# Decoder on one core: the MLP's second products by seven block products, four of them moved into the next slot

## The chip, the cores and the metric

The kernel runs on one core of a Trainium2 chip. The metric is the device time of one execution in microseconds (us). Of the kernel before there are three runs, and one more execution that was taken by the hardware profiler. The engines are called as the profile calls them: PE (TensorE, matrix products and transposes), PEld (its weight loads), DVE (VectorE), ACT (ScalarE), POOL (GpSimd) and SP (SyncE, which only issues DMAs here).

## The reference

`x` has the shape (8, 256, 256): 8 batches of 256 tokens with 256 features, all in float32. Cut to what matters:

```python
x0 = x
for i in range(4):
    x = x + self_attention(layer_norm(x, g1[i], b1[i]), Wq[i], Wk[i], Wv[i], Wo[i], bo[i])
    h = layer_norm(x, g2[i], b2[i])
    x = x + (gelu(h @ W1[i] + bias1[i]) @ W2[i] + b2_[i])     # 256 -> 1024 -> 256
x = layernorm(x0 + x)
x = layernorm(x + cross_attention(x, context, xWq, xWkv, xWout, xbout))
C1 = compose(fc1_logits, fc1_A, fc1_B)    # weighted sum of 32 low-rank products, 256 x 1024
C2 = compose(fc2_logits, fc2_A, fc2_B)    # the same, 1024 x 256
x = layernorm(x + gelu(x @ C1) @ C2)
```

Four of the eight heads of the self-attention are local (a causal softmax over a window of 128), and four are linear (softmax of q, elu + 1 of k, sums over buckets of 64). Cross-attention has 16 heads of 64 and 120 context tokens for each batch.

The part that the change touches is the product of `gelu(...)`, 256 x 1024, with `W2`, 1024 x 256, for each batch and layer. It is called the second product below, and the one with `W1` is the first product.

## The kernel before, in words

**Units and slots.** The work is cut into units of one batch and one layer: attention units 0 to 31 and MLP units 0 to 31, then 8 units of cross-attention and 8 units `Composed` of the last MLP. A unit keeps its batch's `x` (two tiles of 128 tokens by 256 features) in SBUF. The main loop (L1365 to L1496) has slots s = 1 to 32. A slot interleaves the second half of attention unit s-1 (`old`), the first half of attention unit s (`new`), MLP unit s-4 (`ff`), and the normalisation and transposition for attention unit s+1 (`after`). In slots 1 to 12 the composed weights are made as well. When they are done, in slot 13, the pools of that work are closed and a pool `cross` is opened; `filled` is true up to there. A second loop (L1506 on) runs cross-attention unit s beside an MLP unit or a `Composed` unit, up to s = 10: MLP units 29 to 31 for s = 0 to 2, `Composed` units 0 to 7 for s = 3 to 10.

**What sets the order.** Each engine runs its own queue in the order in which the program issues instructions; nothing reorders them. So the order of the calls in the loop is the order on each engine, and it is written out by hand. Waits between engines are put in by the framework from the tiles that are read and written. A tile is taken from a pool with a fixed number of buffers, and taking one waits until the buffer's last readers are done. PSUM has eight banks, four in `ps_s` (`bank_s`, L168) and four in `ps_g` (`bank_g`, L171).

**A slot's steps, by line.**
- `qkv` of `new` (L687): q and k transposed (L693, copies on ACT at L701 and on DVE at L702); then, for each of the two tiles w, k, q and v (L713), the copy of v on ACT (L720), the maximum of q and its subtraction on DVE (L725, L726), and the parts of elu + 1 of k on DVE (L732, L733). Between w = 0 and w = 1 it calls `between`; in before that is the normalisation of the next MLP unit (`centre`, L195).
- `linear_sums`, `divide_c`, `turn_p` and `values` of `old` (L809 to L893): the linear heads' sums, the transposes of the softmax weights `p` (L860) with their copies on ACT and, for the last head, DVE (L863, L865), and the products with v.
- `turn` and `turn_sums` of `ff`: transposes of the normalised x (L214), scale and shift on DVE (L223) and ACT (L224), and sums `tx` on POOL (L574 to L577).
- `scores` of `new` (L735): the products (L744), then on DVE for each head the causal mask (L753) and two row maxima (L757).
- The first product of `ff`. It already goes by seven block products in before: with 2 x 2 blocks for both factors, seven products of blocks and some sums of blocks give what eight products give. A block product is four matmuls 128x128 with 128 columns (`one`, L593). `p16`, `p5`, `p27`, `p34` (L608 to L636) are products 1 and 6, 5, 2 and 7, 3 and 4, with their copies (L612, L620, L622), the adds L614, L628 and L633 on DVE and the GELUs on ACT (L918), which end with four blocks `h[11]`, `h[12]`, `h[21]`, `h[22]` of 128 features x 4 x 128 tokens. `first_sums` forms the sums of the blocks of `W1` once for each layer on POOL (L560 to L563).
- `out` of `old` (L895): the projection (L239) and its addition to x (`add_to`, L231, L233).
- The exponentials of `new`: of `qs` and `ke` (L763, L764), then two for each head (`head_exps`, L769, L775). ACT loads a table when it changes from GELU to the exponential or back.
- The second product of `ff` (`second`, L638, L645): 8 matmuls 128x256 for one token tile (`second(1)`), the transposes for `after`, 8 matmuls for the other tile (`second(0)`), and then one addition to x on DVE (L233).
- `softmax_q`, `totals` and `divide` of `new` (L784 to L807), all on DVE: elu + 1 of k (L786), the softmax of q (L788 to L790), the reciprocals of the sums of `p` (L799, L800) and four divisions, one for each head (L805).

`add_bias` (L229) adds a bias to x on POOL. `moments` and `centre` are the two halves of a layer norm: mean and variance on DVE with the reciprocal root on POOL (L189), and the normalisation on DVE (L195). `load_attn` and `load_mlp` issue the weights' DMAs of the next layer on ACT's queue. In the second loop `Pair` makes keys and values of the context by seven products, `Cross` has the attention itself, and `Composed` is an MLP unit with composed weights, whose result is normalised one tile at a time and sent out on SP's queue (L973, L976).

In the names of tiles in the profile, `_a` is an attention unit, `_m` an MLP unit, `_f` a Composed unit; `x`, `h`, `p`, `qs`, `kf` are the tensors named above. A float32 matmul shows as two MATMUL records in the trace, a transpose as one.

## Time and profile before

| | us |
|---|---|
| runs of the kernel before | 1213.03, 1210.98, 1212.82 |
| median | 1212.82 |
| the profiled execution, by its own time | 1211.44 |
| its span in the profile | 1209.7 |
| first qk matmul of slot 13 / of slot 31 | 413.5 / 873.3 |
| length of a slot between these (18 slots) | 25.4 in most, 25.5 on average |
| first cross slot begins | 937.6 |
| length of a cross slot, s = 3 to 7 | 28.6 |

The rows of the profile read as follows. A line of a timeline has the start and the length in us of a run of neighbouring instructions, the engine, the line in the kernel, the operation, what it writes and reads, the shape and the number of instructions; in brackets stands the idle time before it and what ended that. A line of the table of windows has a stretch of the span, and then the busy time of each engine in it.

### The profile page before, as it was taken

How to read it: one execution, taken by the hardware profiler on the slowest of the kernel's cores; microseconds unless marked ns; L12 is line 12 of the kernel's file. 1: busy time of each engine (PE TensorE's matmuls, PEld its weight loads, DVE VectorE, ACT ScalarE, POOL GpSimd, SP SyncE). 2: the span in 40 equal slices, each digit the busy share in tenths (PEclk: the TensorE clock that was granted, in tenths of full speed). 3: DMA queues.
4: the chain of work that ended last, by engine and by line, in shares of the span. 5: the costliest groups of instructions: out<-in, count | busy, mean ns of one | idle time of the engine just before them, and what ended most of it. 6: DMA issues, size and time to landing. Idle time of an engine off the chain costs nothing. (4 is left out here: it accounts for less than half of the span.)

```text
span 1209.7 us, 24149 instructions
## 1 busy us (share of the span) xinstructions
PE 1193.1 (99%) x9117; PEld 956.4 (79%) x9117; DVE 867.1 (72%) x2446; ACT 645.9 (53%) x1794; POOL 457.7 (38%) x687
## 2 busy tenths in 40 slices
PE   8999999999999999999999999999999999999998
PEld 5556788888888888887888878888877777777797
DVE  6878788777878777777877777787774556666643
ACT  4444555554445567766667666677663343333323
POOL 6665455555564322222422222243234324232220
PEclk9999999999999999999999999999999999999999
DMA  5624131110310030010001002020000000000000
GB/s 160 209 85 120 45 92 46 32 31 27 119 45 1 16 111 2 1 47 29 2 1 40 1 2 75 2 70 27 10 10 1 10 9 16 21 9 9 9 15 23
DMA packets 29508, 47.83 MB, mean 40 GB/s; under 512 B 3151, under 2 KB 22735, under 8 KB 29135
## 3 DMA queue, kind: packets, MB, share of 16 engines
q0 software_dynamic: 6656, 20.98, 6.0%
q10 hardware_dynamic: 13024, 14.07, 3.5%
q1 hardware_dynamic: 9710, 11.23, 3.0%
q8 instruction: 72, 1.18, 0.4%
q14 instruction: 46, 0.37, 0.1%
HBM read 44.17 MB, written 2.10 MB: 38 GB/s over the span
## 5 line engine op out<-in xcount | busy, mean ns | idle before, releaser
L645 PE MATMUL ps_p_m<-w,h_m 128*128 128x256 f32 x1024 | 233.3, 380 | 0.0
L645 PEld LDWEIGHTS ps_p_m<-w,h_m 128*128 128x128 f32 x1024 | 189.2, 190 | 22.8
L229 POOL TENSOR_TENSOR x<-x,b 128x256 f32<-128x256 f32 x64 | 48.3, 775 | 221.0 <-DVE xn_m L195 221.0
L713 PE MATMUL qkv_a<-wa,xT_a 128*128 128x512 f32 x256 | 115.1, 592 | 0.0
L775 ACT ACTIVATE p_a<-sc_a,nm_a 128x128 f32<-128x128 f32 (+1 forms) x256 | 103.9, 431 | 2.2 <-DVE nm_a L757 2.0
L713 PEld LDWEIGHTS qkv_a<-wa,xT_a 128*128 128x128 f32 x256 | 48.6, 190 | 47.6 <-issue 45.9
L757 DVE TENSOR_REDUCE nm_a<-sc_a 128x1 f32<-128x128 f32 (+1 forms) x256 | 79.6, 352 | 4.4
L918 ACT ACTIVATE h_m<-h_m,cols 128x128 f32<-128x128 f32 x256 | 78.4, 406 | 0.0
L229 POOL TENSOR_TENSOR x<-x,bo 128x256 f32<-128x256 f32 x64 | 48.2, 774 | 73.3 <-DVE xn_a L195 73.3
L300 POOL DMA_INDIRECT ga<-in_L_ffn_fc_A_dram,idx_a x64 | 62.2, 973 | 24.0 <-issue 15.6
L596 PE MATMUL ps_h_m_a<-xT_m,w 128*128 128x128 f32 x512 | 70.6, 281 | 0.5 <-DVE xT_m L223 0.5
L720 ACT COPY v<-qkv_a 128x256 f32<-128x256 f32 x64 | 23.9, 373 | 84.4 <-PE qkv_a L713 84.4
L596 PE MATMUL ps_h_m_u<-tx_m,w 128*128 128x128 f32 x512 | 67.7, 275 | 0.0
L596 PEld LDWEIGHTS ps_h_m_a<-xT_m,w 128*128 128x128 f32 x512 | 62.4, 191 | 5.3 <-issue 1.9
L239 PE MATMUL ps_p_a<-wo,oT_a 128*128 128x256 f32 x256 | 65.6, 381 | 0.0
L805 DVE TENSOR_TENSOR p_a<-p_a,psum_a 128x384 f32<-128x384 f32 x128 | 63.8, 560 | 1.1
L596 PEld LDWEIGHTS ps_h_m_u<-tx_m,w 128*128 128x128 f32 x512 | 62.3, 192 | 0.0
L693 PE MATMUL ps_qk_a<-xT_a,wa 128*128 128x256 f32 x256 | 60.7, 380 | 0.9 <-ACT aw L354 0.9
L645 PE MATMUL ps_p_f<-w2c,h_f 128*128 128x256 f32 x256 | 57.8, 379 | 0.0
L753 DVE TENSOR_TENSOR sc_a<-sc_a,causal 128x256 f32<-128x256 f32 x128 | 54.3, 424 | 3.3 <-PE sc_a L744 2.1
L387 PE MATMUL ps_w<-gbt,at 128*128 128x512 f32 x128 | 56.7, 596 | 0.0
L775 ACT ACTIVATION_READ_ACCUMULATOR p_a<-sc_a,nm_a 128x1 f32 x256 | 55.9, 218 | 0.0
(312 smaller groups left out, 2742.1 us busy)
## 6 DMA issues: line engine op xcount, KB each, us to landing
w<-in_L_attn_W_dram ACTq DMA_DIRECT2D x8, 1024.0 KB, 6.3
xwkv<-in_L_xattn_Wkv_dram SPq DMA_DIRECT2D x1, 2048.0 KB, 10.2
x_c<-in_x_dram SPq DMA_DIRECT2D x8, 256.0 KB, 2.7
out_dram<-y_f SPq DMA_DIRECT2D x16, 128.0 KB, 1.7
x<-in_x_dram ACTq DMA_DIRECT2D x6, 256.0 KB, 3.5
ga<-in_L_ffn_fc_A_dram,idx_a POOLq DMA_INDIRECT x64, 3.4
xwq<-in_L_xattn_Wq_dram SPq DMA_DIRECT2D x1, 1024.0 KB, 4.8
xwo<-in_L_xattn_Wout_dram SPq DMA_DIRECT2D x1, 1024.0 KB
```

What stands on the lines that cost most here:

```text
L229: nc.gpsimd.tensor_add(xb[:, i, :], xb[:, i, :], bias)
L239: nc.tensor.matmul(ps[:, i * D : (i + 1) * D], lhs(c, i), w[:, c, :], start=c == 0, stop=c == n_in - 1,)
L300: nc.gpsimd.indirect_dma_start(out=dst, out_offset=None, in_=table, in_offset=bass.IndirectOffsetOnAxis(ap=idx, axis=0),)
L387: nc.tensor.matmul(ps, self.at[k][:, m * P : (m + 1) * P], self.b[k][:, n * 512 : (n + 1) * 512], start=k == 0, stop=k == PG - 1,)
L596: nc.tensor.matmul(ps[:, f * P : (f + 1) * P], self.ws[n][:, f * P : (f + 1) * P], self.rhs[n], start=start and f == 0, stop=stop and f == ...
L645: nc.tensor.matmul(self.ps[:, i * D : (i + 1) * D], self.h[k][:, f, :], self.w2[:, half * 4 + f, :], start=k in (11, 22) and f == 0, stop= ...
L693: nc.tensor.matmul(ps[s], wa[:, c, s * HW : (s + 1) * HW], xT[:, c, :], start=c == 0, stop=c == NC - 1,)
L713: nc.tensor.matmul(t, xT[:, c, w * P : (w + 1) * P], wa[:, c, 2 * HW :], start=c == 0, stop=c == NC - 1,)
L757: nc.vector.tensor_reduce(self.nmax[:, h, w : w + 1], sc[:, s], AX.X, ALU.max, negate=True)
L775: nc.scalar.activation(flat[:, s], sc[:, s], AF.Exp, bias=self.nmax[:, h, w : w + 1], accum_out=self.psum[:, h, w : w + 1],)
L805: nc.vector.tensor_tensor(p, p, self.psum[:, h, :, None].to_broadcast([P, 3, P]), ALU.mult)
L918: nc.scalar.activation(dst[:, f, :], src[:, f * P : (f + 1) * P], AF.Gelu, bias=col("ff", i))
```

## The change

The second product also goes by seven block products in slots 13 to 32, and beside cross-attention for s = 0 to 7: 28 units. The last three Composed units keep `second`, and so do the MLP units of slots 4 to 12. Besides that, the order of the calls is changed around it:

- `second_plain` makes products 1, 4 and 2 in one bank, from the GELU blocks as they are, with the transposes for `after` between 4 and 2. `h_sums` forms four sums of the blocks of h on POOL (128 x 512 each); `w2_sums` forms four sums of the blocks of `W2`, once for each layer, on POOL.
- `take` adds a finished block from PSUM to x on DVE, where before there was one addition for the unit. One block can go to two places of x.
- `second_56` and `second_73`, the products that need the sums, come in the next slot: 6 and 5 between the halves w = 0 and w = 1 of `qkv`, 7 and 3 after w = 1. In slot 32 and in the second loop they have other places, in a cross slot after `out`.
- `softmax_q`, `totals` and `divide` move from the end of the slot into the next slot's `qkv`, behind `second_56`.
- The exponentials of `qs` and `ke` come after those of the heads. The normalisation of the next MLP unit goes from `qkv` to the slot's end. The second half of `xT` for `after` is made on DVE and no longer on ACT. Products 5, 2, 7, 3, 4 of the first product are issued without `out` between them; `out(0)` and `out(1)` follow.
- The banks of `ps_s` are taken in a fixed turn; the bank for q and k comes from `ps_g`.
- In the second loop normalisation and transposes for the next unit come earlier, and Composed units 0 to 4 are sent out with one DMA for both tiles.

```diff
+        def two(self, n, ps, slot, a, start=False, between=None):
+            for f in range(4):
+                nc.tensor.matmul(
+                    ps[:, slot * P : (slot + 1) * P],
+                    a[:, f, :],
+                    self.w2s[n][:, f, :],
...
+        def take(self, blocks, src):
+            x = xs[self.b].rearrange("p i (n d) -> p (i n) d", n=2)[:, blocks, :]
+            nc.vector.tensor_add(x, x, src)
+        def second_plain(self, turn=None, between=None):
+            h = self.h
+            self.ps = bank_g(f"ps_p_{self.name}")
+            self.two(1, self.ps, 0, h[11], True, between)
+            self.two(4, self.ps, 2, h[22], False, between)
+            if turn:
+                turn()
+            self.two(2, self.ps, 1, h[12], False, between)
+        def h_sums(self):
...
+            nc.gpsimd.tensor_add(s1, h[21], h[22])
+            nc.gpsimd.tensor_sub(s2, s1, h[11])
+            nc.gpsimd.tensor_sub(h[21], h[11], h[21])
+            nc.gpsimd.tensor_sub(h[22], h[12], s2)
+            self.hs = {5: s1, 6: s2, 7: h[21], 3: h[22]}
+        def second_early(self):
+            ps = self.ps.rearrange("p (k d) -> p k d", k=4)
+            self.take(slice(0, 1), ps[:, 0:1, :])
+            self.take(slice(0, 3, 2), ps[:, 1:3, :])
+        def second_56(self):
...
+            self.two(6, ps, 0, hs[6])
+            self.take(slice(1, 2), ps[:, None, :P])
+            self.two(5, pd, 0, hs[5], start=True)
+            self.take(slice(3, 4), pd[:, None, :P])
+        def second_73(self):
...
+            self.two(7, ps, 0, hs[7])
+            self.take(slice(2, 4), ps[:, None, :P].to_broadcast([P, 2, P]))
+            self.two(3, pd, 0, hs[3])
+            self.take(slice(1, 2), pd[:, None, :P])
...
         if new and s > 1:
-            new.qkv(nxt_c)
+            def between():
+                late.second_56()
+                old.softmax_q()
+                old.totals()
+                old.divide(range(HL))
+            new.qkv(between if late else None, bank_g if late else bank_s)
+        if late and new:
+            late.second_73()
...
-        if ff:
-            ff.second(1, vsums and (lambda: next(vsums)))
...
+        if cross:
+            ff.w2s = w2s
+            ff.second_plain(after and (lambda: after.turn(alone=True)), vsums and (lambda: next(vsums, None)))
+            ff.h_sums()
+            if ff.b == B - 1:
+                mlp_sums[ff.l + 1] = first_sums(mlp_ws[ff.l + 1][0])
...
+        if new and cross:
+            new.begin_exps()
+            new.head_exps(range(HL))
+            new.exps()
...
-        if nxt_m and after and not filled:
-            nxt_c = nxt_m.centre
-        elif nxt_m:
+        if nxt_m:
             nxt_m.centre()
-        if ff:
+        if cross:
+            late = ff
+            ff.second_early()
+        elif ff:
             ff.second(0)
```

## The prediction

> **What bounds the kernel now.** I read the page first, for the span and the engines' shares; then the table of windows over a slot of self-attention, one of cross-attention, the passage between them and the tail; then the timelines of DVE, ACT and PE over the slot that begins at 642.8, because a share doesn't say who waits for whom.
>
> ```profile
> span 1209.7 us, 24149 instructions
> PE 1193.1 (99%) x9117; PEld 956.4 (79%) x9117; DVE 867.1 (72%) x2446; ACT 645.9 (53%) x1794; POOL 457.7 (38%) x687
> ```
>
> ```profile
> 642.80:668.20 25.40, 25.40 (x223) 21.05 (x223) 19.07 (x58) 17.09 (x52) 6.26 (x11) 1.00 0.14 44
> 1054.00:1082.60 28.60, 28.60 (x149) 21.72 (x148) 18.45 (x49) 9.65 (x16) 9.16 (x19) 1.00 0.06 19
> ```
>
> The second fence is the table of windows: after the window come its length and then PE, PE weight loads, DVE, ACT and POOL busy, and the granted clock. PE is without a gap in both kinds of slot, at a granted clock of 1.00. So PE seems to set the time, and an edit that takes work from PE to gain it, as long as nothing else closes in the same 25.4 us. DVE and ACT (19.07 and 17.09 us) look free; whether they are is seen only in order of time.
>
> ```profile
> 643.73 0.17 DVE L799 COPY psum_a<-psum_a 128x4 f32<-128x4 f32 x1 [2.23 <-ACT p_a L775]
> 644.19 1.96 DVE L805 TENSOR_TENSOR p_a<-p_a,psum_a 128x384 f32<-128x384 f32 x4
> 646.08 0.68 DVE L233 TENSOR_TENSOR x<-x,ps_p_m 128x512 f32<-128x512 f32 x1
> 646.67 0.41 DVE L702 COPY qk_a<-ps_qk_a 128x256 f32<-128x256 f32 x1
> ...
> 647.92 0.72 DVE L195 TENSOR_SCALAR xn_m<-x,mv_m,rs_m 128x256 f32<-128x256 f32 x2
> ...
> 655.70 0.69 DVE L614 TENSOR_TENSOR ps_h_m_u<-ps_h_m_u,h_m 128x512 f32<-128x512 f32 x1
> ...
> 665.44 0.42 DVE L786 TENSOR_TENSOR kf_a<-kf_a,ke_a 128x256 f32<-128x256 f32 x1
> ...
> 669.11 0.17 DVE L799 COPY psum_a<-psum_a 128x4 f32<-128x4 f32 x1 [2.22 <-ACT p_a L775]
> ```
>
> ```profile
> 656.42 0.59 ACT L620 COPY h_m<-ps_h_m_u 128x512 f32<-128x512 f32 x1 [1.83 <-DVE ps_h_m_u L614]
> ...
> 663.39 1.28 ACT L763 ACT_TABLE_LOAD   x1
> 664.68 0.42 ACT L763 ACTIVATE qs_a<-qs_a 128x256 f32<-128x256 f32 x1
> ...
> 666.90 0.57 ACT L224 ACTIVATE xT_a<-ps_t_a,cols 128x256 f32<-128x256 f32 x1
> ...
> 668.84 0.24 ACT L775 ACTIVATION_READ_ACCUMULATOR p_a<-sc_a,nm_a 128x1 f32 x1
> ```
>
> Here is a second closed ring. The last exponential of the heads (ACT, L775) releases the totals (DVE, L799) at 643.73. DVE has no gap over 0.2 us until the add L614 ends at 656.38: 12.65 us. That add releases the ACT copy L620 at 656.42, and from there ACT runs without a gap through the GELUs, the change of table and the exponentials to 669.08, and releases the next totals at 669.11: 12.69 us. 12.65 + 12.69 and the handover give 25.38, PE's own period. So two rings have the same length, and taking work from PE gains only if the other becomes shorter too.
>
> **What PE gains.** A unit's old second products are 16 matmuls 128x256 (each two records):
>
> ```profile
> 659.99 1.06 PE L596 MATMUL ps_h_m_u<-tx_m,w 128*128 128x128 f32 x8
> 660.88 3.62 PE L645 MATMUL ps_p_m<-w,h_m 128*128 128x256 f32 x16
> ```
>
> From start to start, 16 records of 256 columns take 3.46 us (660.88 to 664.34), so 16 matmuls take 6.92; 8 records of 128 columns take 0.89 (659.99 to 660.88), so the 28 matmuls 128x128 of seven products take 6.23. PE gains 0.69 us for a unit, and a slot of PE's alone would be 25.38 - 0.69 = 24.69. The 24 more weight loads of a unit cost nothing more, as the first products, all of the small kind, hold 0.89 with theirs.
>
> [...]
>
> **What the DVE part of the ring becomes.** In the changed order the ring is no longer closed by the totals. DVE's copy of qk (L702) waits for ACT's half of the same copy (L701), and ACT's order puts that behind the eight head exponentials and behind the exponentials of qs and ke, which were moved to the end. So DVE's part of the ring runs from the qk copy to the end of L614. Against the 12.65 us:
> - Out: the add L233 of the second products, 0.59 (646.08 to 646.67); the normalisation xn_m, 0.69 (647.92 to 648.61, now at the slot's end); the small wait before the masks, which is filled, 0.17.
> - In: the additions of products 6, 5, 7 and 3. Three are 128x128 from PSUM, 0.21 each by the spacing of L726, which has that size; one is 128x256, 0.34 by the spacing of L702: 0.97.
> - In: the four instructions of softmax_q (L786 to L790), now between the two halves of qkv. In before they lie beside ACT's exponentials, where DVE waits anyway (2.22 us in the last DVE row). Their spacing from 640.05 is 0.34 + 0.45 + 0.24 + 0.34 = 1.37.
>
> Sum: 12.65 - 1.45 + 0.97 + 1.37 = 13.54, so 0.89 more.
>
> **What the ACT part becomes.** Out: the second half of xT_a, 0.45 (666.90 to 667.35), now on DVE in a place where it waits for ACT anyway. The last exponential's accumulator read and its signal (668.84 to 669.11, 0.27) are no longer at the end; the qk copy is, 0.38 and 0.03 for the signal. Sum: -0.31. The qs and ke exponentials only change places.
>
> **The new period** is 25.38 + 0.89 - 0.31 = 25.96 us, against 24.69 for PE alone. PE then has 1.27 us of gaps in a slot; I expect them before product 7, which waits for DVE's addition of product 6 (same bank), and before ps_t_m, which waits for the addition of product 3.
>
> **The sum over slots 13 to 30** (first qk matmul from 413.5 to 873.3 us, 459.8 in all; mean 25.54, since slots 14, 18 and 26 wait 0.47 for a bank and 28 to 30 carry 1.6 of work on the context):
> - 18 x 25.96 = 467.3. I count the three bank waits as gone, since PE has gaps now.
> - Work on the context in slots 28 to 30: 0.6, as part of 1.6 now lies in PE's gaps.
> - POOL beside DVE. The sums of h (four POOL 128x512 a unit, 1.29 each by L433's mean in the page) and the bias addition behind them (1.51) end near softmax_q, whose first and last instructions read two operands in SBUF. Bounds for a slot: nothing, if they end before, and 0.4, if both instructions and one division lose what the rows below show. I take 0.1, as the overlap is short: 1.8 in all.
> - Slots 19 and 27: first_sums (4 POOL 128x512 at 1.27 to 1.36, 5.2 us) now stand behind the sums of h, and so beside the divisions and ahead of the bias addition. Bounds 0.9 (four divisions) and 2.5 (half of the 5.2 in PE's way): 1.5 each, 3.0.
> - Slots 13 and 21: the seven DMA issues of load_attn, on ACT's queue, took from 641.10 to 644.60. Nothing waited for them; now the qk copy stands behind them. They began 2.5 us before the last exponential ended, so about 1.0 is left over: 2.0. The three issues of load_mlp (some 1.5) fit into those 2.5.
> - Slot 13: w2_sums (four POOL 128x512, 5.2 us) start behind compose.final, which ends at 420.2; the sums tx of the MLP then come at about 425.5 to 426.6, and product 6 needed them at 424.4. Between 0.5 and 2.2: 1.4.
>
> 476.1 against 459.8: **16.3 us lost**.
>
> ```profile
> 900.95 2.83 DVE L805 TENSOR_TENSOR p_a<-p_a,psum_a 128x384 f32<-128x384 f32 x4
> ```
>
> This is the nearest row for POOL beside DVE: while POOL forms tx (L576 and L577, 0.77 us instead of 0.46), the four divisions take 2.83 us instead of 1.96, so 0.22 each.
>
> [...]
>
> **What is gained elsewhere.**
> - Cross slots: eight units at 0.69 = 5.5. PE is gapless there (28.60 of 28.60), and DVE and ACT (18.45 and 9.65) have room: the additions add 0.4, the sums 5.2 us to POOL's 9.16 of 28.60.
> - From slot 31 to the first cross slot (873.3 to 937.6), PE is busy for 61.73 of 64.3. Two units save 1.4 there, but slot 31 still has the long ring; some of the gaps are filled by the matmuls moved there. Net 0 to 2.5: 1.2.
> - The tail from 1168.4: the last Composed units get their transposes and first products earlier; gaps of 0.42 and some of 0.2 before products 4 and 7 go: 1.2 of 41.3 (0 to 2).
>
> That is 7.9 us. **Sum:** 16.3 - 7.9 = 8.4 over the profiled execution, 1211.44 (span 1209.7, 1.7 around it): 1219.8, so 1220. The median of the runs shown is 1212.82, 1.4 higher; on that scale it would be 1221.
>
> **The rivals.**
> - *The ring is 25.96, but its company is hidden* (POOL's sums, the DMA issues, slot 13). Then 467.3 + 0.6 - 459.8 - 7.9 = +0.2: 1211.6, no change. For it: most of these terms have nothing as a lower bound. Against it: the DMA issues stand on ACT, through which the ring runs.
> - *PE stays the bound, and the kernel is faster.* The place is the qk copy of DVE. If it isn't held by ACT's copy, because ACT gets there early or the wait is void, then the copy, the first half's four instructions and the first two additions (0.34 + 0.91 + 0.42) lie beside the exponentials; DVE's part is 11.87 and the ring about 24.3, below 24.69. It decides from there: as soon as the ring is under 24.69, each period is PE's. 18 x 0.69 = 12.4, less slot 13's 1.4, and with the 7.9: 18.9 less, 1192.5. Against it: ACT has no gap between L620 and the last exponential, and the copy is behind them all.
> - *The ring lies in between*, since starts of neighbouring instructions move closer in another order. At 25.4 to 25.6 it is 457 to 461, with 3 us of the extra terms: 1204 to 1208.
> - *More waits than I count*: product 6 waits for POOL's second sum, which I put at 1 us before it is needed, and each division loses time to POOL in every slot. At 0.6 us more a slot the time is 1220 + 11 = 1231.
>
> **Chances.** The forecast (1214 to 1226) 0.50; its company hidden 0.14; PE the bound 0.12; in between 0.12; more waits 0.12. Faster by over 0.2% (the 2.4 us that a measurement of this kernel can tell from no change) is 0.24, within it 0.14, slower 0.62. The range runs from 1201, which leaves out PE as the bound, to 1233, which takes in most of the last rival; the likeliest case's own range is 1214 to 1226.
>
> **What would show it.** Right: a period of 25.9 to 26.3 us between first qk matmuls of slots 14 to 30; PE gaps of about 1.3 us in a slot, before product 7 and ps_t_m; DVE's L702 waiting for ACT, then DVE without gaps to the add of p16; cross slots of 27.9. Wrong: PE gapless in slots 14 to 30 with a period near 24.7, or PE waiting for POOL before product 6. If the period is 25.96 and the total is not, the terms of single slots were mis-sized.

## The result

The changed kernel is **slower**: 1251.61 us (median of 1252.12, 1251.41, 1251.80 and 1248.09) against 1212.07 us for the kernel before on the same chip (four runs). The ratio is 1.0325, with a 95% interval of 1.0312 to 1.0337. The forecast was 1220, with a range from 1201 to 1233, so the sign was right and the size was a fifth of what came: +8.4 was worked out, +40.7 came (profiled executions, 1252.12 against 1211.44).

The page of the changed kernel has more work on every engine but ACT, and a longer span:

```profile
span 1250.4 us, 25871 instructions
PE 1208.5 (97%) x9789; PEld 979.2 (78%) x9789; DVE 961.4 (77%) x2593; ACT 634.1 (51%) x1777; POOL 613.8 (49%) x810
```

The table of windows over a steady slot, over slot 20 and over a cross slot (length, then PE, weight loads, DVE, ACT, POOL, and the granted clock):

```profile
709.00:735.60 26.60, 25.64 (x248) 21.48 (x247) 22.43 (x65) 16.21 (x50) 11.06 (x16) 1.00 0.01 2
597.40:628.70 31.30, 28.89 (x249) 23.21 (x248) 25.87 (x65) 16.66 (x51) 21.87 (x24) 0.89 0.01 2
1114.00:1142.20 28.20, 28.20 (x170) 22.13 (x171) 21.90 (x53) 9.95 (x18) 14.41 (x22) 1.00 0.03 11
```

A steady slot now lasts 26.66 us from first qk matmul to first qk matmul (25.38 before), and three slots stand out: 20 with 31.27, 28 with 31.80, 30 with 31.56. In slot 20 POOL is busy for twice the time of the steady slot, and the mean clock is 0.89. In the steady slot DVE and ACT show where the period is closed. DVE first:

```profile
709.18 2.35 DVE L199 TENSOR_SCALAR xn_m<-x,mv_m,rs_m 128x256 f32<-128x256 f32 x2
...
712.79 0.42 DVE L785 COPY qk_a<-ps_qk_a 128x256 f32<-128x256 f32 x1 [0.60 <-ACT qk_a L784]
...
714.63 0.93 DVE L871 TENSOR_TENSOR kf_a<-kf_a,ke_a 128x256 f32<-128x256 f32 x1
...
716.95 1.96 DVE L890 TENSOR_TENSOR p_a<-p_a,psum_a 128x384 f32<-128x384 f32 x4
...
726.25 0.69 DVE L621 TENSOR_TENSOR ps_h_m_u<-ps_h_m_u,h_m 128x512 f32<-128x512 f32 x1
```

```profile
712.34 0.42 ACT L784 ACTIVATE qk_a<-ps_qk_a 128x256 f32<-128x256 f32 x1
712.64 0.38 ACT L803 COPY v<-qkv_a 128x256 f32<-128x256 f32 x1
...
727.02 0.59 ACT L627 COPY h_m<-ps_h_m_u 128x512 f32<-128x512 f32 x1 [2.06 <-DVE ps_h_m_u L621]
```

This is the ring of the prediction: the qk copy on DVE waits for ACT, then DVE has no gap over 0.2 us up to the end of L621 (712.79 to 726.94, 14.15 us), and ACT needs 12.44 from the start of L627 to the release of the next qk copy at 739.46. What doesn't fit is one length: the addition L871 takes 0.93, and the same addition took 0.42 in before. POOL's row shows what lies beside it:

```profile
712.63 1.27 POOL L701 TENSOR_TENSOR h_m<-h_m,h_m 128x512 f32<-128x512 f32 x1
713.87 1.40 POOL L236 TENSOR_TENSOR x<-x,b 128x256 f32<-128x256 f32 x2
```

The last sum of h and the two additions of the bias run from 712.63 to 715.27. L871 has both inputs in SBUF, starts at 714.63, ends at 715.55 and is the only one of its run that is longer; its neighbours that read PSUM keep their 0.28. So what lies beside it here is the second half of the bias addition, which the four sums have pushed back; the sums themselves lie beside xn_m and the PSUM reads. The xn_m ahead of the ring (2.35 for two instructions that took 0.72) is held too, but in time in which DVE would wait for ACT anyway.

In slot 20 the sums for the next layer's W1 stand behind the sums of h on POOL. DVE beside them:

```profile
605.18 1.23 DVE L884 COPY psum_a<-psum_a 128x4 f32<-128x4 f32 x1
606.44 0.23 DVE L885 RECIPROCAL psum_a<-psum_a 128x12 f32<-128x12 f32 x1
606.70 3.78 DVE L890 TENSOR_TENSOR p_a<-p_a,psum_a 128x384 f32<-128x384 f32 x4
```

A copy of 128x4 takes 1.23 instead of 0.16, and four divisions take 3.78 instead of 1.96. PE waits behind them in four gaps between 607.1 and 611.8 (2.36 us in all): two for the divisions (1.38), one for ACT's copy of their transposes (0.55) and one for DVE's additions (0.43). The clock falls at 610.8. The windows of this stretch, the clock in the third column from the end:

```profile
609.00:611.00 2.00, 1.39 (x9) 0.98 (x9) 1.97 (x6) 0.90 (x3) 0.69 (x2) 0.95 0.00 0
611.00:613.00 2.00, 1.57 (x10) 0.89 (x9) 1.86 (x11) 0.19 (x1) 0.00 (x0) 0.50 0.03 8
613.00:615.00 2.00, 2.00 (x28) 1.32 (x32) 1.37 (x4) 0.56 (x1) 0.80 (x2) 0.50 0.00 0
615.00:617.00 2.00, 2.00 (x45) 1.41 (x38) 1.93 (x7) 0.58 (x2) 2.00 (x4) 0.50 0.02 4
```

For 6.8 us the clock is 0.50. Half of that, 3.4 us, is my upper estimate of its cost; compared record by record with a steady slot, and without the gaps, PE's work in this stretch takes 2.6 us longer. So it goes in slots 28 and 30 (2.5 and 2.7), and behind slot 31 there are two more stretches, of 3.4 and 6.8 us. In all PE loses some 8 us to the clock in the three slots and up to 5.1 behind them; the kernel before has no such stretch ahead of its end.

**Where the time came from**, by the first matmuls of each stage:

| stretch | before | after | change | forecast |
|---|---|---|---|---|
| slots 13 to 30 | 459.8 | 492.3 | +32.5 | +16.3 |
| slot 31 to the first cross-attention output | 86.9 | 92.8 | +5.9 | -1.2 |
| first to eighth cross-attention output | 197.6 | 196.4 | -1.1 | -5.5 |
| the rest | | | +3.4 | -1.2 |

The forecast's stages were cut a little earlier than these, at the start of the cross slots. The last row is no loss: four products of a unit (3.57 us) now lie behind the last marker, and slot 13, at the start of the first row, has four fewer.

What PE does in a steady slot, as sums of the distances from start to start of its records, by groups (the last column is the kernel of the last experiment):

| group | before | after | last experiment |
|---|---|---|---|
| q, k, v | 5.25 | 5.20 | 5.20 |
| second products | 6.91 | 6.34 | 6.34 |
| first products | 6.35 | 7.60 | 6.45 |
| transposes of p | 1.31 | 1.67 | 1.31 |
| products with v | 1.26 | 1.51 | 1.43 |
| all others | 4.30 | 4.36 | 4.30 |
| sum | 25.39 | 26.67 | 25.03 |

The second products do gain 0.57 of the 0.69 forecast. The first products lose 1.25. Of it 0.73 is one wait: their product 7 waits for ACT's copy behind the ring. The rest is in smaller delays around it.

```profile
725.97 1.06 PE L603 MATMUL ps_h_m_a<-xT_m,w 128*128 128x128 f32 x8
727.75 1.13 PE L603 MATMUL ps_h_m_u<-tx_m,w 128*128 128x128 f32 x8 [0.73 <-ACT h_m L627]
```

### The profile page after: what moved, and what is told of

Its sections match the earlier page's. It is cut to its first block, busy times and chain, and to the rows that moved or that the text cites. A ratio compares the mean times of both kernels' runs of the same rounds, so it can differ in the third digit from the quotient of the medians.

```text
span 1250.4 us, 25871 instructions
## 1 busy us (share of the span) xinstructions
PE 1208.5 (97%) x9789; PEld 979.2 (78%) x9789; DVE 961.4 (77%) x2593; ACT 634.1 (51%) x1777; POOL 613.8 (49%) x810
## 4 chain that ended last, share of the span: by engine, by line
PE 73%; DVE 20%; ACT 3%; issue 2%; POOL 1%; ACTq 0%; POOLq 0%; DVEq 0%
PE ps_p_m L668 6%; PE ps_h_m_u L603 6%; PE qkv_a L796 6%; PE ps_p_m L652 5%; PE ps_w L394 4%; PE ps_p_a L246 4%; PE ps_qk_a L776 4%; PE ps_w L456 4%; DVE p_a L890 4%; PE ps_h_m_d L603 3%; PE ps_h_m_a L603 3%; DVE nm_a L840 2%; PE ps_xq_c L1268 2%; PE ps_y_c L1352 2%; DVE sc_a L836 2%
## 5 line engine op out<-in xcount | busy, mean ns | idle before, releaser
L796 PE MATMUL qkv_a<-wa,xT_a 128*128 128x512 f32 x256 | 118.1, 592 | 0.0
L193 POOL TENSOR_TENSOR rs_m<-rs_m,neghalf 128x2 f32<-128x2 f32 x32 | 22.5, 704 | 136.8 <-DVE rs_m L188 136.8
L668 PEld LDWEIGHTS ps_p_m<-t,h_m 128*128 128x128 f32 x552 | 70.8, 195 | 18.9 <-issue 15.8
L603 PE MATMUL ps_h_m_u<-tx_m,w 128*128 128x128 f32 x512 | 70.5, 281 | 11.8 <-ACT h_m L627 10.9
L581 POOL TENSOR_TENSOR tx_m<-xT_m 128x128 f32<-128x128 f32 x32 | 14.6, 455 | 132.1 <-DVE xT_m L227 132.1
L668 PE MATMUL ps_p_m<-t,h_m 128*128 128x128 f32 x552 | 75.3, 279 | 0.2 <-DVE x L682 0.2
L890 DVE TENSOR_TENSOR p_a<-p_a,psum_a 128x384 f32<-128x384 f32 x128 | 68.5, 596 | 1.1
L652 PE MATMUL ps_p_m<-w,h_m 128*128 128x256 f32 x288 | 65.1, 379 | 0.0
L246 PE MATMUL ps_p_a<-wo,oT_a 128*128 128x256 f32 x256 | 62.1, 380 | 0.0
L193 POOL TENSOR_TENSOR rs_a<-rs_a,neghalf 128x2 f32<-128x2 f32 x32 | 22.8, 711 | 73.3 <-DVE rs_a L188 73.2
```

The source lines that it names most:

```text
L246: nc.tensor.matmul(ps[:, i * D : (i + 1) * D], lhs(c, i), w[:, c, :], start=c == 0, stop=c == n_in - 1,)
L603: nc.tensor.matmul(ps[:, f * P : (f + 1) * P], self.ws[n][:, f * P : (f + 1) * P], self.rhs[n], start=start and f == 0, stop=stop and f == ...
L652: nc.tensor.matmul(self.ps[:, i * D : (i + 1) * D], self.h[k][:, f, :], self.w2[:, half * 4 + f, :], start=k in (11, 22) and f == 0, stop= ...
L668: nc.tensor.matmul(ps[:, slot * P : (slot + 1) * P], a[:, f, :], self.w2s[n][:, f, :], start=start and f == 0, stop=f == 3, skip_group_che ...
L796: nc.tensor.matmul(t, xT[:, c, w * P : (w + 1) * P], wa[:, c, 2 * HW :], start=c == 0, stop=c == NC - 1,)
L890: nc.vector.tensor_tensor(p, p, self.psum[:, h, :, None].to_broadcast([P, 3, P]), ALU.mult)
```

## The experiments

**The theory** after the result: the ring was as forecast, but POOL's sums, and the bias addition behind them, hold up DVE's instructions that work within SBUF, 0.5 us in each slot and several us where more sums stand behind them, and gaps of PE that lie close together halve its clock. **Rivals:** the ring itself was summed wrongly; the moved softmax alone does it; PE's small matmuls cost more than their rows say.

The names in brackets are those by which the expectations call each other. The experiments ran on several chips. On three of them (experiments 1 to 9) slots 1 to 12 of every profiled kernel are some 11 to 17 us longer in all, and the kernel before takes 1224 to 1228 us there; times are compared with before on the same chip, and slots 13 to 30 with each other.

**1. No sums on POOL** (e1). This kernel leaves out the four sums of h: the products take the GELU blocks in their place.

```diff
-            nc.gpsimd.tensor_add(s1, h[21], h[22])
...
-            self.hs = {5: s1, 6: s2, 7: h[21], 3: h[22]}
+            self.hs = {5: h[21], 6: h[22], 7: h[21], 3: h[22]}
```

> The changed kernel without the four sums of h on POOL: products 5, 6, 7 and 3 take blocks of h as they are, so the second products' result leaves these sums out. Theory (the ring of DVE and ACT closes the slot, and POOL's long sums hold up DVE's softmax_q beside them): a steady slot goes from 26.66 to about 26.0 us, the ring that the prediction worked out; the weight sums of slots 20, 28 and 30 start 5.2 us earlier and are done before the divisions, so these slots lose their 4.6 to 5.1 us too; in all 1251.6 - 0.6 x 17 - 14 = about 1227 us. Rival (PE itself is slower with the small products, by weight loads and waits inside the groups): a steady slot stays at 26.6, and only the three single slots may gain: 1237 or more.

Measured: 1239.98 against 1226.97, ratio 1.0112 (1.0093 to 1.0131). The steady slot is **26.12**; slots 20, 28 and 30 are 26.68, 27.14 and 27.33; one clock drop is left, behind slot 31. DVE's rows:

```profile
717.63 0.42 DVE L780 COPY qk_a<-ps_qk_a 128x256 f32<-128x256 f32 x1 [2.21 <-ACT qk_a L779]
...
719.49 0.42 DVE L866 TENSOR_TENSOR kf_a<-kf_a,ke_a 128x256 f32<-128x256 f32 x1
```

The addition is back at 0.42, and the period falls by 0.54. The bias addition now ends 1.6 us ahead of the qk copy. So the ring without the sums is 26.12, where 25.96 was worked out, and POOL's company costs the rest and most of the three long slots. The sums could also have held PE itself, which needs their results; in the changed kernel's slots 13 to 30, though, PE waits for POOL only once (0.5 us, for tx). Without the sums the kernel is 13.0 us over before; with them, on another chip, it was 39.5 over. So about a third of the loss is left without them (18 slots at 0.74 more are 13.3), and the sums, with the clock drops that they bring, have the rest.

**2. The layer's sums behind the divisions** (e2). `first_sums` and `column_sums` wait for the last division through a one-column instruction on POOL.

```diff
+            gate = small.tile([P, 1], F32, tag="gate", name=f"gate_{s}")
+            nc.gpsimd.tensor_add(gate, old.p[-1][:, 2, 0:1], old.p[-1][:, 2, 0:1])
+            mlp_sums[held] = first_sums(mlp_ws[held][0])
```

> The changed kernel with first_sums (slots 20 and 28) and the first column_sums (slot 30) held on POOL until the last division of the slot is done; all else is the same. Theory (the weight sums block the divisions, PE runs dry for some 2.4 us, and the granted clock of PE then falls to half for 7 us): these three slots come to 27 us from 31.3, 31.8 and 31.6, the clock stays at 1.00 in them; 1251.6 - 14 = 1237 us. If only the blocking goes and the clock still falls: about 1247. Rival (the slots are long because of the DMA loads or the in-place sums of a layer's weights): no change, 1251.

Measured: 1260.63 against 1226.97, ratio 1.027 (1.0255 to 1.0286). Slots 20, 28 and 30 are 28.63, 29.04 and 29.30, 2.3 to 2.8 less than in the changed kernel, but not the 27 that I expected. POOL and DVE in slot 20:

```profile
623.87 1.26 POOL L568 TENSOR_TENSOR s<-s,w 128x512 f32<-128x512 f32 x1
625.22 1.29 POOL L569 TENSOR_TENSOR s<-w,s 128x512 f32<-128x512 f32 x1
```

```profile
620.23 1.97 DVE L890 TENSOR_TENSOR p_a<-p_a,psum_a 128x384 f32<-128x384 f32 x4
...
624.04 1.13 DVE L931 TENSOR_SCALAR rk_a<-cs_a 128x3 f32<-128x3 f32 x1
625.20 0.17 DVE L932 RECIPROCAL rk_a<-rk_a 128x3 f32<-128x3 f32 x1
625.41 1.22 DVE L934 TENSOR_TENSOR cn_a<-cs_a,rk_a 128x96 f32<-128x96 f32 x1
```

The divisions are free again. Now a scalar addition of 128x3 takes 1.13 instead of 0.17, and a product of 128x96 takes 1.22 instead of 0.26; the reciprocal between them keeps its 0.17. So here the hold isn't a matter of how much an instruction moves: both take 0.96 longer than by themselves, and they end at 625.17 and 626.63, where the POOL sums beside them end at 625.13 and 626.51. The clock is 1.00 in slots 20 and 28, and the 2.6 and 2.8 us that these slots gain are about what PE's work took longer at half clock (2.6 and 2.5); PE's gaps are no shorter (2.8 us in slot 20, 2.4 in the changed kernel), the waits have only moved on. In slot 30 the clock still falls, for 3.4 us.

**3. The softmax moved alone** (e3). The kernel before with `softmax_q`, `totals` and `divide` moved into `qkv`, and `second` as it was.

```diff
+            def between():
+                if owed:
+                    owed.softmax_q()
+                    owed.totals()
+                    owed.divide(range(HL))
+                if mlp_c:
+                    mlp_c()
```

> The kernel before, with softmax_q, totals and divide moved behind the first half of the next slot's qkv in slots 13 to 30; the second products are as before. Theory (the cover of softmax_q beside ACT's exponentials is given up, and DVE's qk copy becomes the head of the ring): DVE's part is 12.65 + 1.37 - 0.59 - 0.17 = 13.26, ACT's 12.69 - 0.27 + 0.41 = 12.83, a slot of 26.1 against 25.38, and 1212 + 17 x 0.7 = 1224 us. Rival (PE bounds the slot and DVE has room): 25.4 and 1212, no change.

Measured: 1282.59 against 1226.97, ratio 1.0451 (1.0435 to 1.0467), with a slot of 28.63. My expectation missed. From q, k and v to the products with v PE takes 3.2 us longer than in before, as it waits for DVE at each step behind the divisions:

```profile
744.73 0.53 PE L818 MATMUL ps_c_a<-v,kf_a 64*32 64x33 f32 x24 [0.22 <-DVE kf_a L786]
745.67 0.44 PE L828 MATMUL ps_q_a<-ident,qs_a 128*128 128x128 f32 x2 [0.41 <-DVE qs_a L790]
746.70 2.22 PE L860 MATMUL ps_pT_a<-ident,p_a 128*128 128x128 f32 x12 [0.59 <-DVE p_a L805]
```

In the changed kernel the four late products (3.57 us) stand in this place. That they fill the time, so that the two halves of the change need each other, I take from the two orders; no run shows it alone. The waits of PE are a cost that neither forecast nor theory had counted.

**4. Seven products beside cross-attention alone** (e4). Slots 13 to 32 as in before; `second_plain`, `h_sums` and the late products only in the second loop.

```diff
-            ff.second_plain(after and (lambda: after.turn(alone=True)), vsums and (lambda: next(vsums, None)))
+            ff.second(1, vsums and (lambda: next(vsums)))
```

> Slots 1 to 32 as in the kernel before, and the second products by seven block products only beside cross-attention, with the second loop of the changed kernel. Forecast on record: 0.69 us less for each of 8 units, 1212 - 5.5 - 1.2 = 1205 us. Theory by the trace of the changed kernel: its cross slots gained only 0.3 to 0.4 each, and the slot with the sums of the composed weights lost 2.2: 1212 - 2.5 + 2 = 1211 us, within 2 us of no change.

Measured: 1227.74 against 1226.97, ratio 1.0003 (0.9993 to 1.0013): no change, where the forecast has -5.5 for this part. Undisturbed cross slots are 28.2 to 28.45 instead of 28.62 (the first, from output to output, 28.17 instead of 30.16). Slot s = 3 has 32.51: there `w2_sums` for the composed weights stands on POOL beside the shares of cross-attention, PE gets a gap of 2.2 us, and here the clock falls behind it for 3.4 us. In the changed kernel the same slot has a gap of 2.1 us, keeps its clock and takes 30.82.

**5. The softmax back at the slot's end** (e5), and with it the normalisation in `qkv`, all else as changed.

```diff
-                old.softmax_q()
-                old.totals()
-                old.divide(range(HL))
+                if mlp_c:
+                    mlp_c()
```

> The changed kernel with softmax_q, totals and divide back at the slot's end, the exponentials of qs and ke ahead of the heads' again, and the normalisation of the next MLP unit back between the halves of qkv; the products of the seven stay where the change put them. If the lost cover of softmax_q were the whole cost (the mechanism on record): DVE's part 12.65 - 0.59 + 0.97 - 0.17 = 12.87, ACT's 12.69 - 0.45 = 12.24, a slot of 25.1. Theory after the first runs (each DVE instruction that works on SBUF alone waits for the POOL sum that is under way, up to 1.3 us): the four sums of h, from 6 to 1 us before the last exponential and past it, now stand beside softmax_q and the divisions, so the stall only moves there, divisions take over 2.5 us instead of 1.96 and the slot is 26.3 to 26.9; no better than the change's 26.66.

Measured: 1284.73 against 1227.97, ratio 1.0464 (1.0448 to 1.048); the slot is 27.40. That is more than the 26.3 to 26.9 expected, and slots 20, 28 and 30 have 33.0 to 33.7. The divisions now meet the four sums of h (2.73 instead of 1.96) and DVE's addition of product 6 comes so late that PE waits 1.23 us ahead of product 7. The ring alone was put at 25.1; how much of the 2.3 us above it is POOL's, beyond the 0.77 at the divisions, isn't shown.

**6 and 7. POOL out of the way** (e6, e7). Softmax of q on POOL, divisions at the slot's end, the fourth sum of h and the layer's sums behind the divisions or spread over slots; in 6 the normalisation goes on ACT, in 7 it stays on DVE.

```diff
+                new.totals()
+                new.divide(range(HL))
+                ff.gate(new.p[-1])
+            ff.h_sum3()
```

> As the run before, but with POOL kept away from DVE: the first three sums of h go ahead of the root of the MLP's variance, beside DVE's moments and the copies from PSUM; elu + 1 of k and the last step of softmax_q run on POOL; the fourth sum of h waits for the last division; the normalisation of the next MLP unit runs on ACT, in its idle time between the two copies of v; first_sums and column_sums go out two instructions a slot behind the sums tx, beside the masks, and the sums of the composed weights wait for the last weighing of v. Theory: DVE's part 12.87 - 0.69 + 0.2 = 12.4, ACT's 12.24, a ring of 24.6, so PE bounds the slot at 24.7 to 25.0, no clock below 1.00 from slot 14 to 31, and the kernel is 18 x 0.5 + 3 = 12 us faster than before on the same chip (8 to 15). Rival (PE pays for the small products with stalls inside its groups, 25.4 in the change's slot without its two gaps): 25.4 and 0 to 3 us faster.

> As the run with POOL out of the way, with the normalisation of the next MLP unit on DVE between the halves of qkv, not on ACT. Theory: DVE's part has 0.7 - 0.2 more, a ring of 12.87 + 12.24 = 25.1 and a slot of 25.1 to 25.3. Rival (DVE isn't in a closed ring any more): the same as the run before.

Measured: 1247.96 and 1248.81 against 1227.97, ratios 1.0162 (1.0147 to 1.0178) and 1.0175 (1.0159 to 1.019). The slots are 26.38 and 26.43, and 20 and 28 are as short as the others: the clock stays at 1.00 from slot 13 to slot 31. But the steady slot hardly moved. The expectation of 6 missed with its rival (25.4); in 7 the rival came, no difference from 6. Of PE in the seventh:

```profile
717.43 2.01 PE L794 MATMUL ps_qk_a<-xT_a,wa 128*128 128x256 f32 x8 [0.34 <-DVE xT_a L227]
735.47 1.13 PE L614 MATMUL ps_h_m_u<-tx_m,w 128*128 128x128 f32 x8 [0.49 <-ACT h_m L638]
```

PE has only these two gaps over 0.2 us, so most of what is left is in smaller delays: the first products take 7.37 there and the second 6.89, against 6.35 and 6.91 in before. Two suspects: the addition of product 6, which product 7 waits for, and `out`, which no longer stands between the first products.

**8 and 9. The additions first** (e10, e11). PE makes qk, w = 0 and then products 6 and 5, and DVE adds them ahead of its copies; in 8 two divisions come behind these additions, in 9 all four are done before.

```diff
+                if between and w == 0:
+                    between(0)
+                    take_qk()
```

> As e7_xn_on_dve, but in qkv PE forms qk and w = 0 first and then the products 6 and 5, and DVE adds 6 and 5 to x ahead of its copy of qk and of the copies of w = 0; the divisions of heads 2 and 3 come behind these additions instead of ahead of them. So product 7 finds its bank free. If the ring DVE addition -> products 7 and 3 -> scores -> adds -> exponentials is what holds e7 at 26.4, the steady slot falls to 24.8 to 25.3, the gap of 0.49 before product 7 is gone, and the time is 2 to 8 us under the kernel before. Rival: what is left in e7 is POOL's lock on DVE (L188 at 1.12), which this order does not touch: then the slot stays at 26.1 to 26.5 and the time 17 to 23 us above before.

> As e10_takes_first, but all four divisions stay at the end of the slot before, ahead of the additions. By the ring theory DVE still reaches the additions before PE has made the products: 24.8 to 25.3, as in e10_takes_first within 0.2. If the 1.0 us of two divisions ahead of the additions decides, the slot is 25.5 to 26.3.

Measured: 1255.61 and 1240.72 against 1224.37, ratios 1.0259 (1.0245 to 1.0273) and 1.0142 (1.0126 to 1.0157). The slots are 26.71 and **25.82**. So the place of two divisions is worth 0.9 us, and it is 9 that is better, against the expectation; 8 is above both of its cases. Not all of 9's 16 us over before are in its slots: behind slot 31 the clock is at 0.50 for 17 us, in three stretches. DVE in 9, from the totals to the add behind the scores:

```profile
710.37 0.17 DVE L910 COPY psum_a<-psum_a 128x4 f32<-128x4 f32 x1 [2.06 <-ACT p_a L886]
710.58 0.23 DVE L911 RECIPROCAL psum_a<-psum_a 128x12 f32<-128x12 f32 x1
710.84 2.60 DVE L916 TENSOR_TENSOR p_a<-p_a,psum_a 128x384 f32<-128x384 f32 x4
...
723.26 0.69 DVE L632 TENSOR_TENSOR ps_h_m_u<-ps_h_m_u,h_m 128x512 f32<-128x512 f32 x1
```

The ring of before is back, closed by the totals that wait for the last exponential: 13.58 on DVE and 12.24 on ACT are 25.82. DVE's part is 0.93 longer than before's 12.65: 0.64 is POOL's company on the divisions, and the rest the additions, less what went out.

**10. The order of the copies alone** (e13). The changed kernel, with DVE's half of the qk copy issued ahead of ACT's.

```diff
-            nc.scalar.mul(self.qk[:, 0, :], ps[0], DH**-0.5)
             nc.vector.tensor_copy(self.qk[:, 1, :], ps[1])
+            nc.scalar.mul(self.qk[:, 0, :], ps[0], DH**-0.5)
```

> The changed kernel with one edit: DVE's half of the copy of qk is issued ahead of ACT's half, so that ACT's waits for DVE's and not the reverse. The prediction's ring is closed at this copy. The copies of w = 0 on DVE still wait for ACT's copy of v, which stands behind the same exponentials. Ring theory: only the copy itself (0.42, and its signal) goes out of DVE's part, so the steady slot falls by 0.3 to 0.5 to 26.1 to 26.4. Rival: the copy is what closes the ring, so that without its wait PE's own work decides and the slot falls to 25.5 or less. Slots 20, 28 and 30 stay 3 to 5 us longer than the others by both.

Measured: 1251.48 against 1211.13, ratio 1.0335 (1.0319 to 1.0351), with a slot of 26.67. Neither case: no gain at all.

```profile
711.76 0.42 DVE L784 COPY qk_a<-ps_qk_a 128x256 f32<-128x256 f32 x1
712.89 0.29 DVE L808 TENSOR_REDUCE qm_a<-qkv_a 128x4 f32<-128x128 f32 x1 [0.71 <-ACT v L803]
```

The copy no longer waits. The next instruction does, for ACT's copy of v. In the changed kernel that copy ends at 713.02, and the maximum L808 starts at 713.13, so without the first wait it could have started at most 0.11 us earlier. The ring is closed by two waits, and to take one is to take none.

**11. Both waits taken, and the divisions inside `qkv`** (e12). Products 5 and 6 come right behind qk; DVE copies qk and takes w = 0 ahead of ACT, and totals and divisions come behind w = 0. POOL has its four sums and the softmax of q done by then. `out` goes back between the first products.

```diff
+            if between and wait:
+                between(0)
+                take_qk()
...
+                elif i == 1:
+                    old.totals()
+                    old.divide(range(HL))
+                    if mlp_c:
+                        mlp_c()
+                else:
+                    late.second_73()
...
-            if cross:
-                ff.p5()
-                ff.p27()
-                ff.p34()
...
+            old.out(0)
+            ff.p5()
+            ff.p27()
+            old.out(1)
+            ff.p34()
```

> What e11_takes_first_all_divided still loses is, by its trace, a ring on DVE and ACT: from the totals that wait for the last exponential (710.37) DVE is gapless to the add behind the scores (723.95), 13.58, and ACT needs 12.24 from there to the next last exponential; and 0.49 of PE before product 7. Here the totals and divisions come behind the copies of w = 0, DVE copies qk before ACT does and takes w = 0 ahead of ACT's copy of v, so that DVE adds 5 and 6 and copies qk beside the exponentials; POOL has its four sums and the softmax of q done before the divisions start; and out goes back between the first products. Theory: the ring falls below PE's own work, the slot is 24.7 to 25.2 with no PE gap above 0.3 except where weights are loaded, and the time is 3 to 12 us under the kernel before. Rival: a slot of seven products can't be brought under that of before, because POOL's four sums of h lock out DVE wherever they stand: the slot stays at 25.6 to 26.4 and the time at 10 to 20 us above.

Measured: 1217.32 against 1211.13, ratio 1.0051 (1.0037 to 1.0065). The slot is **25.03**, below that of before, as expected; the time isn't. Two places outside the slots lose it: the cross slots are 28.8 to 29.05, since product 7 now follows the addition of 6 at once (a gap of 0.47 in each), and at the end of slot 31 the normalisation waits behind the exponentials:

```profile
895.08 1.14 PE L218 MATMUL ps_t_m<-ident,xn_m 128*128 128x128 f32 x4 [4.58 <-DVE xn_m L199]
```

**12. These two places mended** (e14).

```diff
+            if not five:
+                self.two(6, ps, 0, hs[6])
+                self.take(slice(1, 2), ps[:, None, :P])
...
+            if cross and new and not after:
+                nxt_m.centre(bias=False)
```

> As e12_divide_in_qkv with two places outside slots 13 to 30 mended. Beside cross-attention product 6 comes ahead of 5 again, so that product 7 doesn't follow the addition of 6 at once: e12's cross slots of 28.8 to 29.1 should become 28.1 to 28.4 again, 4 to 5 us in all. At the end of slot 31 the normalisation of the next MLP unit comes before the sums of h and isn't held by the exponentials, and in slot 32 the totals and divisions stand behind products 6, 5, 7 and 3: the PE gaps there (4.6 and 1.5 us in e12, with a clock of 0.50 behind them for 3.4 us) should shrink to 1 to 3 us. The slots stay at 25.03. Theory (the losses of e12 are these two places): 6 to 11 us under e12, so 0 to 5 us under the kernel before. Rival (the passage is bound by the exponentials whatever stands there): only the 4 to 5 us of the cross slots, and the time within 2 us of before.

Measured: **1206.39** against 1211.22, ratio **0.9959** (0.9946 to 0.9973): as expected, and 0.4% faster than before, which is little, but its whole interval lies below 1. Slots 13 to 30 take 451.1 (459.8 in before), the cross slots are 28.1 to 28.5, and the passage takes 90.5 where before has 86.9. Up to 5.1 of that are clock (0.50 from 914.1 to 924.4). The window of a steady slot, and POOL and DVE in it:

```profile
663.30:688.33 25.03, 25.03 (x247) 21.55 (x247) 19.78 (x62) 16.37 (x50) 12.51 (x18) 1.00 0.00 1
```

```profile
666.28 1.26 POOL L720 TENSOR_TENSOR h_m<-h_m,h_m 128x512 f32<-128x512 f32 x1
667.51 0.72 POOL L909 TENSOR_TENSOR kf_a<-kf_a,ke_a 128x256 f32<-128x256 f32 x1
668.19 0.61 POOL L913 TENSOR_TENSOR qs_a<-qs_a,qsum_a 128x256 f32<-128x256 f32 x1
672.09 1.52 POOL L236 TENSOR_TENSOR x<-x,b 128x256 f32<-128x256 f32 x2 [3.29 <-DVE xn_m L199]
```

```profile
669.72 1.97 DVE L928 TENSOR_TENSOR p_a<-p_a,psum_a 128x384 f32<-128x384 f32 x4
671.60 0.73 DVE L199 TENSOR_SCALAR xn_m<-x,mv_m,rs_m 128x256 f32<-128x256 f32 x2
```

PE is gapless, with POOL as busy as in the changed kernel (12.51 against 11.06). POOL's run ends at 668.8, DVE's divisions and normalisation lie from 669.72 to 672.3, and POOL's next one starts at 672.09: of DVE's none is held. So with this order the seven products do pay. It has several edits in it, and no run shows what each alone is worth.

## Why the prediction fell short

**The step that failed** is "POOL beside DVE", put at 0.1 us in a slot with bounds of 0 and 0.4. Measured are 0.54 (26.66 less 26.12 without the sums), outside the bounds: 18 slots make 10 us and not 1.8. The upper bound was also added up too low: two instructions and one division at the row's 0.22 are 0.66, and 0.51 if the two, of 256 elements against the division's 384, lose in proportion; 0.54 would have been at or within that, and not outside 0.4. But the price was of the wrong kind. It was a mean over four divisions, taken once for each instruction; here one instruction waits for nearly all of what is left of a POOL instruction, 0.51 of the 0.54 on L871 alone, beside the bias addition. In experiment 2 the product of 128x96, with two inputs in SBUF, took 1.22 for 0.26. The rows show the same for instructions with one tensor in SBUF, of which the prediction did not speak: 1.13 for 0.17 at 128x3, 1.23 for 0.16 at 128x4. Reads of PSUM (0.28 and 0.29 beside the bias addition) and reciprocals (0.23 in slot 20) did not wait. A whole sum of 1.29 us in each slot would have been too much, though: in the steady slot L871 starts 0.64 ahead of the end of the bias addition, and loses 0.51.

**A term was missing:** the clock. Some 8 us in three slots, and up to 5.1 behind slot 31, are PE at half clock: between a fifth and a third of the loss. The prediction read the clock as 1.00 everywhere and never asked what PE's new gaps would do to it. A slot with `first_sums` was put at 1.5 more, with bounds of 0.9 and 2.5; it was 4.6 and 5.1 more, of which 2.6 and 2.5 is clock, so 2.0 and 2.7 without it, the second with work on the context in it. `column_sums` in slot 30 wasn't counted at all; that slot is 4.9 longer, of which 2.7 is clock. A fall of the clock didn't cost the same everywhere: 3.4 us of it made slot s = 3 longer by 1.6 or 1.7 (32.43 and 32.51 in experiments 10 and 4, against 30.82), but a slot of experiment 3 only by 0.2 (28.8 against 28.63).

**Point by point.**
- *Two closed rings, so PE's gain alone brings nothing:* right. Experiments 9 and 11 show both rings again.
- *PE gains 0.69 in a unit:* 0.57 in a slot, 0.66 beside cross-attention (6.92 to 6.26).
- *The ring is 25.96, closed by DVE's qk copy, which waits for ACT:* right within 0.16 (26.12 without the sums). DVE has 14.15 where 13.54 was worked out, 0.51 of it L871; ACT's part is 12.44, 0.25 less than before, where 0.31 was said. That the qk copy is the place was half of it: the copy of v is another, 0.11 us behind (experiment 10).
- *PE's gaps before product 7 of the second products and ps_t_m, 1.27 in all:* some 0.96, of which only 0.2 is before ps_t_m; the large gap (0.73) lies before product 7 of the first products. The sign of being wrong, PE waiting for POOL before product 6, did not come.
- *The three bank waits go:* right in slots 18 and 26.
- *load_attn, 1.0 each:* 0.3 (slots 14 and 22, 26.98 and 26.97).
- *Slot 13, 1.4 more:* it was 1.65 less, 23.74 against 25.39, since its own late products lie in slot 14. This was an oversight.
- *Cross slots, -5.5:* -1.1. The undisturbed ones gain 0.27 to 0.42 instead of 0.69, as other groups, the first products most of all (0.14), give back 0.24 in the slot at 1114, the first gains 2.1, and s = 3 loses 2.2 (30.82) through `w2_sums`.
- *The passage, -1.2:* +5.9, of which up to 5.1 is clock.
- *The rivals:* "more waits" had the mechanism, "each division loses time to POOL in every slot", at 0.6 a slot. It was not the divisions (1.96 in the steady slot, as before) but one addition, so the size was right by luck. "PE stays the bound" would not have needed one wait to be void but two (experiments 10 and 11).

Added up: of 32.3 us between forecast and result, 16.2 are in slots 13 to 30 (10.8 period, 11.7 long slots, less 1.4 and 4.3 for load_attn and slot 13, less 0.6 on the context), 7.1 in the passage, 4.4 in the cross slots and 4.6 in the rest, which is mostly the shifted marker.

**What stays open.** PE's slot of 25.03 in the last kernel is 0.34 above the 24.69 worked out for PE alone. The groups say where (0.12 in the second products, 0.17 in the products with v, 0.10 in the first products, less 0.05 in q, k and v), but not why. The passage behind slot 31 still loses 3.6 us to that of before. There the clock falls without a gap ahead of it, while PE alternates second products with matmuls of 8 columns for the context. This came in nine of the eleven kernels whose second products have 128 columns there (all but experiments 1 and 5; in the changed kernel at 959.0, in experiments 2, 6, 9 and 10 at 967.8, 957.4, 944.7 and 956.9, with PE busy all through the 3.41 us ahead), and in none of the three where they have 256 (before, experiments 3 and 4). So it seems to be a price of the split itself; no run took it away alone.

## What to carry to other kernels

Work moved to POOL is not free because POOL is idle: list the DVE instructions that will lie beside it, and price those that work within SBUF by a row in which such a one was held, and not by a mean. Here those of 0.16 to 0.26 us by themselves took 0.96 to 1.07 more beside POOL sums of 1.26 to 1.33 (reciprocals and reductions weren't held: 0.23 and 0.41 in slot 20). Where two rings are equally long, follow every wait that closes the new one, for taking one of two waits gained nothing (26.67 against 26.66 in experiment 10), and an order that separated POOL's run from DVE's SBUF work turned a loss of 3% into a gain of 0.4%. And where a change opens gaps in a PE that had none, look at the clock behind them: in slot 20 its fall cost 2.6 us, and the added gaps 1.5.

## What the runs showed of the hardware

- **The clock fell behind gaps of PE, and behind slot 31 without one.** In the 3.41 us ahead of four drops of the changed kernel PE was busy for 36 to 57% (51% ahead of 610.8). Around the gap of 2.1 us at 1076 it was busy for 49% of the 3.41 us that end at 1078.4, and the clock stayed at 1.00; in experiments 4 and 10 the same place had 35 and some 40%, and it fell. In experiment 3 it fell behind some 65% (at 604.5, 891.3 and 949.3) and stayed at 1.00 behind as much (at 689.9), so no threshold comes out of these runs. The stretches at 0.50 last 3.4, 6.8 or 10.2 us (610.8 to 617.6 in the changed kernel, 944.7 to 954.9 in experiment 9), and the starts and ends of the five in the changed kernel all lie whole multiples of 3.413 us apart. One drop (959.0) followed 3.41 us in which PE was never idle, but ran four matmul records of 8 columns between every two of 128.
- **A DVE instruction of 0.17 us took 1.13** beside POOL (128x3, experiment 2). In the whole trace of the changed kernel scalar additions (L931, 0.17 to 0.99), copies (L884, 0.16 to 1.26), products (L934, 0.26 to 1.19) and sums within SBUF (L871, 0.41 to 0.93) were held in some slots; the maximum read from PSUM (L808, 0.28 to 0.29), the reduction L873 (0.40 to 0.41) and the reciprocals L874, L885 and L932 (0.20, 0.23 and 0.18) kept their times in all.
- **Splitting matmuls of 256 columns into twice as many of 128 cost PE little in itself**: 112 to 113 ns a record (6.26 and 6.34 us for 56) against 216 (6.92 for 32), in slots and beside cross-attention, with 24 more weight loads a unit.
